# Gate/up units from inner products only: seven of seven outer products split, two units run as seven interleaved pairs, ScalarE seeds PSUM with running sums

## The chip, the cores and the metric

The kernel runs on one core of a Trainium2 chip. The metric is device time in microseconds (us) of one launch, the median of several runs. Engine names are those of the profile: PE is TensorE's matmul stream and PEld its weight loads, DVE is VectorE, ACT is ScalarE, POOL is GpSimd, and SP is the engine whose queue issues nearly all DMAs. Everything is fp32.

## The reference

One layer: a layer norm, then linear attention and a mixture-of-experts feed-forward block on the same normed input, both added to the residual. The change touches the gate and up projections of the feed-forward block only:

```
xn = layernorm(x)                                  # x: 2 x 1024 x 512
w  = routing weights of 8 experts, two kept        # sigmoid scores, top 2
gate = xn @ W_gate + lora(xn, shared) + sum_e w_e * lora_e(xn)   # 512 -> 1376
up   = xn @ W_up   + the same with its own factors
hidden = silu(gate) * up
out  = hidden @ W_down + ...                       # 1376 -> 512
x + attention(xn) + out
```

The shared low-rank factors are folded into the weights; the experts' factors stay as a matmul with a contraction of 64 rows (8 experts by rank 8).

## The kernel before

**Stages.** Up to 236 us of the profile the kernel norms and transposes x, does keys, queries, routing and the odd columns of the feed-forward block. From 236.2 to 512.1 us it does the gate and up projections. After that it does the down projection, the attention output and the residual.

**A unit.** The middle stage has ten units: five pairs of 128-column blocks `j` of the weights, times two batches `b` of 1024 tokens. A unit has to form a 2 by 2 block product (gate and up by two halves, 512 tokens by 512 tokens, contraction 512). It uses the Strassen-Winograd scheme: seven outer products `p` = 1 to 7 in place of eight. An outer product is itself a 2 by 2 block product. Five of the seven (1, 6, 2, 5, 3) are again done with seven inner products each (class `Inner`): 35 matmuls of 128 rows by 128 columns over 256 tokens. The other two (7 and 4) are done plainly by `product`: 8 matmuls over 512 tokens, accumulated in the held PSUM banks `b0` and `b1`. Eight matmuls over 512 tokens and 64 rows (`low_rank`) add the experts' part, into the banks `b`, `x` and `y`. In fp32 every matmul is two instructions on PE.

**Inner.** Inner product numbers 1 to 7 are weights `WI` times tokens `TI`; 1 and 2 use raw blocks, the others sums of blocks. Products 1, 6, 5 and 3 run up one PSUM region `ua`: after each of them ACT copies the running sum into an SBUF tile `r`, and the next accumulates on it. Products 7 and 4 run up a second region `lo`, product 2 has its own region `x_`. DVE adds `x_` and twice `lo` to the tiles. So PE may overwrite `ua` only when ACT has copied it, and may put product 4 on `lo` only when DVE has added product 7 from it:

```
        def c_sum(self):
            nc.vector.tensor_add(self.r[1][:, H1], self.r[1][:, H1], self.lo)

        def d(self):
            self.mm(self.lo, 4)
```

**Order.** PE, DVE, ACT and POOL are scheduled by hand: each runs its instructions in the order in which the program writes them (`manual_schedule`). `unit` writes the order of a unit out: inner products of two outer products alternate, with plain products and low-rank matmuls between. DVE then adds the outer products together (`add`, L1290, 128 by 512, most with both inputs in SBUF, some with one in PSUM), multiplies silu(gate) by up (L1278), and SP stores the result `h` to DRAM.

**Sums for the inner products.** Token sums are made once for each batch and outer product, weight sums once for each `j`. `next_pair(j)` hooks the work for the next `j` into the units: `fold_pe` (PE, contraction of 8 rows) and `fold_adds` (DVE, L978) fold the shared factors into the weights, `fold_sums` (DVE, L982 to L985, 128 by 256) makes the outer weight sums, `inner_weight_sums` (L1182 to L1185) the inner ones, for outer products 1, 5 and 6 on DVE and for 3 and 2 on POOL. Of the token sums, those for batch 0's products 1, 5 and 6 are made on DVE ahead of the stage, the rest on POOL in the first unit (L1138, L1160 to L1163).

**Banks.** PSUM has eight banks in this stage: `held0` to `held3`, `ab0`, `ab1`, `x0`, `x1`.

Of the kernel before, what the change touches and what calls it, by code (L numbers as in the profile page):

```python
# [10 lines left out]
F32 = mybir.dt.float32  # L11
# [4 lines left out]
P = 128  # L16
# [21 lines left out]
def layer_kernel(  # L38
# [129 lines left out]
    ad_sb = const.tile([P, FULL + 1, LR], F32, name="ad_sb")  # L168
# [66 lines left out]
    wT = [const.tile([P, BT], F32, name=f"wT{b}") for b in range(NBATCH)]  # L235
# [369 lines left out]
    def weights_across(b):  # L605
# [6 lines left out]
        nc.sync.dma_start(out=w_dram[b].rearrange("e t p -> t e p"), in_=wx)  # L612
        for i in range(2):
            for e in range(E):
                k = i * ER + e * RANK
                nc.sync.dma_start(
                    out=wT[b][k : k + RANK, :],
                    in_=w_dram[b][e].rearrange("t p -> (t p)").partition_broadcast(RANK),
                )
# [513 lines left out]
    def sums_of_four(eng, src, to):  # L1133

        b11, b12 = src[:, :, 0, 0:TH], src[:, :, 0, TH:TB]
        b21, b22 = src[:, :, 1, 0:TH], src[:, :, 1, TH:TB]
        for k, x, y in ((0, b12, b11), (1, b22, to[:, :, 0]), (2, b22, b12), (3, b21, to[:, :, 1])):
            eng.tensor_sub(to[:, :, k], x, y)  # L1138
            yield

    def inner_tokens(b, ps, t):

        for i, p in enumerate(ps):
            raw = tsum[b][p]
            TI[b, p] = {1: raw[:, 0, 0:TH], 2: raw[:, 1, 0:TH], 3: raw[:, 1, TH:TB],
                        4: t(i, 3), 5: t(i, 0), 6: t(i, 1), 7: t(i, 2)}

    def token_sums_56(eng, b, t):
        yield from sums_of_four(eng, tsum_pair[b], t)
        inner_tokens(b, (5, 6), lambda i, k: t[:, i, k])  # L1150

    def token_sums_23(b, t):
        yield from sums_of_four(nc.gpsimd, xnT[b][1].rearrange("p k (g n) -> p g k n", g=2), t)
        inner_tokens(b, (2, 3), lambda i, k: t[:, i, k])

    def token_sums_1(eng, b):
# [7 lines left out]
        inner_tokens(b, (1,), lambda i, k: t[:, k // 2, k % 2])  # L1164

    WI = {}

    def inner_weight_sums(eng, j, ps):

        w = [t.rearrange("p s (k m) -> p s k m", m=P) for t in wsum[j][0]]  # L1170
        if ps == (3,):

            slots_ = slice(5, 6)
            to = [w[k // 2][:, A21 : A21 + 1, k % 2] for k in range(4)]
        else:
            one = ps == (2,)
            slots_ = slice(1, 2) if one else slice(0, 6, 2)
            wi = p3.tile([P, 1, 4, P], F32, tag="wi2", name=f"wi2_{j}") if one else slot(5, [4, 4, P], f"wi{j}")
            to = [wi[:, 0 : len(ps), k] for k in range(4)]
        g, u = (t[:, slots_] for t in w)  # L1180
# [17 lines left out]

    class Inner:


        def __init__(self, j, b, p, tag, n):
            self.of = (j, p), (b, p)
            self.n, self.name = n, f"{p}_{tag}"

        def mm(self, out, n, start=False):
            w, t = WI[self.of[0]][n], TI[self.of[1]][n]
            nc.tensor.matmul(out, w, t, start=start, stop=True, skip_group_check=True)  # L1208

        def a(self):  # L1210
            self.r = [u_tile(f"r{m}_{self.name}") for m in range(2)]
            ab, x_ = (
                ps_pool[0].tile([P, 2, TH], F32, tag=f"{t}{self.n % 2}", name=f"{t}{self.name}") for t in ("ab", "x")
            )
            self.ua, self.lo, self.x_ = ab[:, 0], ab[:, 1], x_[:, 0]

            self.mm(self.ua, 1, start=True)
            nc.scalar.copy(self.r[0][:, H0], self.ua)  # L1218
            self.mm(self.x_, 2, start=True)

        def a_sum(self):
            nc.vector.tensor_add(self.r[0][:, H0], self.r[0][:, H0], self.x_)

        def b(self):
            self.mm(self.lo, 7)
# [953 lines left out]
```

## Time and profile before

| what | value |
|---|---|
| median of 3 runs | 721.93 us (720.92 to 722.11) |
| profiled execution: span from first to last instruction | 719.1 us |
| what lies around the span (median less span; the page gives no total of its own for this execution) | 2.8 us |
| granted TensorE clock | 1.000 |
| PE busy, DVE busy, ACT busy, POOL busy | 99%, 81%, 28%, 20% of the span |
| gate/up stage | 236.2 to 512.1 us: 275.9 us |
| its five column pairs `j` start at | 236.23, 290.30, 344.77, 399.24, 453.70 us |

A matmul's recorded duration runs to its modelled end, which lies after the next matmul's start: the pace of PE is read from the starts of successive matmuls, not from the mean duration. The chain of waits puts 84% of the span on PE and 13% on DVE.

### The profile page before, as it was taken

What the parts mean: (1) busy time and instruction counts of PE and PEld (TensorE: products, weight loads), DVE (VectorE), ACT (ScalarE), POOL (GpSimd) and SP (SyncE); (2) the same over time, 40 slices, a digit from 0 to 9 for tenths busy, and PEclk for the clock granted to TensorE, in tenths of its full rate; (3) what the DMA queues carried; (4) which work ended last, traced back from release to release, by engine and by line L of the source; (5) the groups of instructions that cost most, each with busy time, mean ns of one, the idle gap of its engine ahead of it and who ended that gap; (6) DMA issues with size and microseconds to landing.
All of it is one profiled execution on the core that took longest, in us unless ns stands there. A gap on an engine that the chain in (4) does not pass through costs nothing.

```text
span 719.1 us, 9872 instructions
## 1 busy us (share of the span) xinstructions
PE 712.2 (99%) x3410; PEld 488.9 (68%) x3410; DVE 581.7 (81%) x1331; ACT 198.2 (28%) x438; POOL 143.0 (20%) x176
## 2 busy tenths in 40 slices
PE   8999999999999999999999999999999999999998
PEld 6666675454433666666666566566788899899897
DVE  7888776777688678778778778878988789998884
ACT  4434413553532233233333333333100000000000
POOL 4033011101001842112212211534520100000000
PEclk9999999999999999999999999999999999999999
DMA  6243001115584100310210211343662444533101
GB/s 179 99 139 103 0 1 59 40 33 150 136 225 130 32 31 30 90 61 31 88 59 30 88 52 37 118 145 119 205 198 102 128 161 131 153 105 110 59 16 45
DMA packets 61734, 66.85 MB, mean 93 GB/s; under 512 B 10866, under 2 KB 49522, under 8 KB 61428
## 3 DMA queue, kind: packets, MB, share of 16 engines
q1 hardware_dynamic: 61154, 66.20, 30.1%
q8 instruction: 27, 0.44, 0.3%
q14 instruction: 23, 0.19, 0.1%
q10 hardware_dynamic: 530, 0.02, 0.0%
HBM read 44.11 MB, written 22.09 MB: 92 GB/s over the span
## 4 chain that ended last, share of the span: by engine, by line
PE 84%; DVE 13%; ACT 2%; issue 1%; POOL 0%; DVEq 0%; POOLq 0%
PE ab L1208 16%; PE b L1268 8%; PE po L1956 7%; PE pg L410 5%; PE pqu L781 4%; PE pya L1785 4%; PE pxa L1785 4%; PE pyb L1785 3%; PE ph L1653 3%; PE x L1208 3%; PE pxb L1785 2%; PE pyc L1785 2%; PE pxa L860 2%; PE b L1263 2%; PE pqv L781 2%; PE pr L1095 2%
## 5 line engine op out<-in xcount | busy, mean ns | idle before, releaser
L1268 PE MATMUL b<-t,w 128*128 128x512 f32 x160 | 83.2, 601 | 0.1
L410 PE MATMUL pg<-kt,xn 128*128 128x512 f32 x128 | 58.7, 594 | 0.5 <-DVE kt L354 0.5
L1290 POOL TENSOR_TENSOR r<-r,r 128x512 f32<-128x512 f32 x20 | 29.8, 1511 | 85.5 <-DVE t L1290 83.3
L1208 PE MATMUL ab<-ti,wi 128*128 128x256 f32 x180 | 45.4, 379 | 0.0
L1208 PEld LDWEIGHTS ab<-ti,w 128*128 128x128 f32 x140 | 25.1, 189 | 29.7 <-DVE r L1236 8.5
L1208 PEld LDWEIGHTS ab<-ti,wi 128*128 128x128 f32 x180 | 34.2, 190 | 13.2 <-issue 4.8
L1290 DVE TENSOR_TENSOR r<-r,r 128x512 f32<-128x512 f32 x60 | 43.2, 760 | 0.0
L1208 PE MATMUL ab<-ti,w 128*128 128x256 f32 x140 | 41.2, 387 | 0.8 <-DVE r L1236 0.4
L410 PEld LDWEIGHTS pg<-kt,xn 128*128 128x128 f32 x128 | 23.1, 190 | 22.6 <-issue 20.8
L1236 DVE TENSOR_TENSOR r<-r,ab 128x256 f32<-128x256 f32 x50 | 20.9, 418 | 21.7 <-ACT r L1233 21.0
L1241 ACT COPY r<-ab 128x256 f32<-128x256 f32 x50 | 18.6, 373 | 71.1 <-PE ab L1208 71.1
L1268 PEld LDWEIGHTS b<-t,w 128*128 128x128 f32 x160 | 29.2, 190 | 10.6 <-issue 5.9
L1244 DVE TENSOR_TENSOR r<-r,ab 128x256 f32<-128x256 f32 x50 | 20.9, 418 | 16.4 <-ACT r L1241 15.9
L1218 ACT COPY r<-ab 128x256 f32<-128x256 f32 x50 | 18.7, 374 | 48.4 <-PE ab L1208 47.1
L1956 PE MATMUL po<-wd,f 128*128 128x256 f32 x140 | 30.9, 380 | 0.1
L1229 ACT COPY r<-ab 128x256 f32<-128x256 f32 x50 | 18.6, 373 | 40.7 <-PE ab L1208 40.7
L1956 PEld LDWEIGHTS po<-wd,f 128*128 128x128 f32 x140 | 26.4, 190 | 4.4 <-issue 0.5
L1899 DVE TENSOR_TENSOR f<-f 128x256 f32<-128x256 f32 x84 | 29.4, 419 | 0.1
L1208 PE MATMUL ab<-xnT,w 128*128 128x256 f32 x100 | 29.4, 390 | 0.0
L419 POOL TENSOR_TENSOR ksum<-ksum,kt 128x512 f32<-128x512 f32 x12 | 15.8, 1318 | 63.1 <-DVE lg L456 42.7
L1208 PE MATMUL ab<-xnT,wi 128*128 128x256 f32 x100 | 28.1, 379 | 0.0
L1208 PEld LDWEIGHTS ab<-xnT,w 128*128 128x128 f32 x100 | 18.1, 189 | 10.9 <-issue 5.3
(483 smaller groups left out, 1651.0 us busy)
## 6 DMA issues: line engine op xcount, KB each, us to landing
h_dram<-h SPq DMA_DIRECT2D x40, 256.0 KB
f<-h_dram SPq DMA_DIRECT2D x10, 512.0 KB
x_ring<-in_x_dram SPq DMA_DIRECT2D x16, 256.0 KB
q_dram<-qt SPq DMA_DIRECT2D x16, 256.0 KB
xr<-in_x_dram SPq DMA_DIRECT2D x16, 256.0 KB
out_dram<-xr SPq DMA_DIRECT2D x15, 256.0 KB
w<-in_w_gate_dram SPq DMA_DIRECT2D x10, 256.0 KB
w<-in_w_up_dram SPq DMA_DIRECT2D x10, 256.0 KB
```

Source lines behind the costliest of these rows:

```text
L410: nc.tensor.matmul(pg[m], xns[n][:, ts(m, P)], kt, start=(j == 0), stop=(j == TPBATCH - 1))
L781: nc.tensor.matmul(banks[c], wqs[p][:, k, ts(c, P)], tsum[b][p][:, k, :], start=(start and k == 0), stop=(k == 1), skip_group_check=True,)
L1208: nc.tensor.matmul(out, w, t, start=start, stop=True, skip_group_check=True)
L1218: nc.scalar.copy(self.r[0][:, H0], self.ua)
L1236: nc.vector.tensor_add(self.r[1][:, H1], self.r[1][:, H1], self.lo)
L1244: nc.vector.tensor_add(self.r[1][:, H0], self.r[1][:, H0], self.lo)
L1268: nc.tensor.matmul(pb[m], ws[m][:, A_OF[p], ts(k, P)], tsum[b][p][:, k, :], start=start, stop=True, skip_group_check=True)
L1290: eng.tensor_add(to[m], t[m], v[m])
L1653: nc.tensor.matmul(phs[u][g * ER : (g + 1) * ER, :], a, f[:, g, :], start=(ns[0] == 0 and n == 0), stop=(last and n == len(chunks) - 1), s ...
L1785: nc.tensor.matmul(o, lhsT, rhs, start=first, stop=True, skip_group_check=True)
L1899: op(t[:, at, :], t[:, x_, :], t[:, y, :])
L1956: nc.tensor.matmul(ps[p][:, q, :], lhsT, rhs, start=start, stop=stop, skip_group_check=True)
```

## The change

All seven outer products are now `Inner` objects, so that a unit has 49 inner matmuls over 256 tokens and no plain product. The two units of one `j` (called `a` for batch 0 and `b` for batch 1) are written as seven **runs** of two interleaved outer products each: (a1, a6), (a7, a5), (a2, a4), (a3, b1), (b6, b7), (b2, b5), (b4, b3). A run has 14 **steps**, one inner matmul each, in the order of `STEPS`. The DVE adds of the inner products stand after the steps named in `SUMS`. All else hangs on a step of a run as a hook.

- The accumulation of outer products in PSUM is replaced by seeds: ACT copies a running sum (128 by 512) from SBUF into a held bank, and the low-rank matmuls accumulate onto it. Six such copies a unit, none before.
- The combination takes 4 adds of SBUF tiles on DVE and 2 on POOL, and 8 adds that read a held bank (`read`) on DVE. The multiply by up moves from DVE to POOL (`store`), all but the last two.
- All inner weight sums in the stage move to POOL, those of the first `j` for products 1, 6 and 7 excepted. There are now sums for products 7 and 4 as well. Token sums for products 7 and 4 of both batches are new: three of these four sets stand on DVE inside the first `j`.
- The fold of the next `j` is one group of matmuls after run 1, its DVE adds follow in run 2, `fold_sums` in run 3.
- Tiles: 14 `u` tiles (10 before), `wT` and `ad_sb` now live in pools that are freed before the stage; the routing weights and the down factors are loaded again (`w4`, `ad_4`) behind it, 34 DMAs on SP.

The core of the diff (hooks are written as run: {step: what}; the `return` is that of `next_fold(j)`, `start` is joined to the hooks of the first `j` only, and `end` is the last `j`, with the folds of the down weights):

```diff
     class Inner:
...
+        def banks(self, n):
+            self.ua = spare_bank(f"ab{n}", f"ab{self.name}")[:, H0]
+            x_ = ps_pool[0].tile([P, 2, TH], F32, tag=f"x{n}", name=f"x{self.name}")
+            self.x_, self.lo = x_[:, 0], x_[:, 1]
+
+        def mm(self, n):
             w, t = WI[self.of[0]][n], TI[self.of[1]][n]
+            out = {2: self.x_, 7: self.lo, 4: self.lo}.get(n, self.ua)
+            nc.tensor.matmul(out, w, t, start=n in (1, 2), stop=True, skip_group_check=True)
+            if n in (1, 6, 5, 3):
+                m, h = {1: (0, H0), 6: (1, H0), 5: (1, H1), 3: (0, H1)}[n]
+                nc.scalar.copy(self.r[m][:, h], self.ua)
+
+        def add(self, n):
+            m, h, v = {2: (0, H0, self.x_), 7: (1, H1, self.lo), 4: (1, H0, self.lo)}[n]
+            nc.vector.tensor_add(self.r[m][:, h], self.r[m][:, h], v)
+
+    STEPS = ((0, 1), (1, 1), (0, 2), (0, 6), (1, 2), (1, 6), (0, 7), (0, 5), (1, 7), (1, 5), (0, 3), (0, 4), (1, 3), (1, 4))
+    SUMS = {3: (0, 2), 5: (1, 2), 9: (0, 7), 11: (1, 7), 12: (0, 4), 14: (1, 4)}
+
+    def pair(x, y, hooks={}):
+        two = Inner(*x), Inner(*y)
+        for n, (k, p) in enumerate(STEPS, 1):
+            if n <= 2:
+                two[k].banks(k)
+            two[k].mm(p)
+            if n in SUMS:
+                k, p = SUMS[n]
+                two[k].add(p)
+            for f in hooks.get(n, ()):
+                f()
...
+        prev = {}
+        if before:
+            prev = {
+                1: [before.read(4, "b", (0,)), before.read(3, "x", (0,))],
+                5: [before.read(4, "b", (1,)), before.read(3, "x", (1,))],
+                6: [before.silu(4)], 11: [before.silu(3)], 12: [before.store(4)], 14: [before.store(3)],
+            }
+        run(1, (a, 1), (a, 6), prev)
+        run(2, (a, 7), (a, 5), {
+            1: [a.sum(V, 6, 1)],
+            11: [a.seed("x", 1, (0,))], 13: [a.seed("x", 1, (1,))],
+        })
+        run(3, (a, 2), (a, 4), {
+            1: [a.sum(V, 7, 6), a.sum(G, 6, 5)],
+            6: [a.seed("b", 7, (0,))], 11: [a.seed("b", 7, (1,))],
+            14: [a.low_rank(("x", 0, 0), ("b", 1, 1))],
+        })
+        run(4, (a, 3), (b, 1), {
+            1: [a.read(2, "x", (0,)), a.read(5, "b", (0,))],
+            5: [a.read(2, "x", (1,)), a.read(5, "b", (1,))],
+            6: [a.seed("x", 6, (0,))], 11: [a.seed("x", 6, (1,))],
+            13: [a.silu(2), a.store(2)],
+            14: [a.silu(5), a.store(5), a.low_rank(("b", 1, 2), ("x", 0, 1))],
+        })
+        run(5, (b, 6), (b, 7), {
...
+        run(6, (b, 2), (b, 5), {
+            1: [b.sum(V, 6, 1, (0,)), b.sum(V, 7, 6, (0,))],
+            5: [b.sum(V, 6, 1, (1,)), b.sum(V, 7, 6, (1,))],
...
+        run(7, (b, 4), (b, 3), {
+            1: [b.sum(G, 6, 5), b.read(2, "x", (0,))],
...
+        return {
+            1: {14: [pe]},
+            2: {5: [adds(0), adds(1)], 14: [adds(2), adds(3)]},
+            3: {5: [lambda: fold_sums(j, 0)], 14: [lambda: fold_sums(j, 1)]},
+            5: {14: [w_sums(G, j, (1,))]},
+            6: {1: [w_sums(G, j, (7, 6))], 14: [w_sums(G, j, (3,))]},
+            7: {14: [w_sums(G, j, (2, 5)), w_sums(G, j, (4,))]},
+        }
...
+    start = {
+        1: {1: [all_of(token_sums_of, V, 0, 7, spare0)], 5: [all_of(token_sums_of, V, 0, 4, spare1)]},
+        3: {1: [lambda: token_sums_1(G, 1)],
+            9: [all_of(token_sums_of, V, 1, 7, [ti23[1][:, 6], ti23[1][:, 7], ti_1[:, 6]])]},
+        4: {1: [all_of(token_sums_56, G, 1, ti_1)]},
+        5: {1: [all_of(token_sums_23, G, 1, ti23[1])],
+            14: [all_of(token_sums_of, G, 1, 4, [ti_1[:, 7 + k] for k in range(3)])]},
+    }
...
+    end = both_units(NP - 1, before, {
+        1: {14: [folds[0][0]]},
+        2: {5: [folds[0][1]], 14: loads((load_down, 2, 0))},
...
+        5: {7: [folds[1][0]], 9: [folds[1][1]], 12: [folds[2][0]], 14: [folds[2][1]]},
+        6: {14: [lambda: feature_sums(0, 0)]},
+        7: {12: [lambda: feature_sums(0, 1)], 14: [lambda: feature_sums(0, 2)]},
     })
...
+    for b in range(NBATCH):
+        spread_weights(b, w4[b])
     first_unit(hr0)
```

`V` is DVE and `G` is POOL. `token_sums_of` is four DVE subtractions of 128 by 256 with both inputs in SBUF. `unit`, `product`, `hidden` and `next_pair` are gone.

## The prediction

> **What bounds the kernel now.** I read the busy times first, then the gate/up stage in the table by stretches, then the PE timeline for the pace of a matmul, then the DVE, ACT and POOL timelines for what a late add does to PE.
>
> ```profile
> PE 712.2 (99%) x3410; PEld 488.9 (68%) x3410; DVE 581.7 (81%) x1331; ACT 198.2 (28%) x438; POOL 143.0 (20%) x176
> PE 84%; DVE 13%; ACT 2%; issue 1%; POOL 0%; DVEq 0%; POOLq 0%
> L1290 DVE TENSOR_TENSOR r<-r,r 128x512 f32<-128x512 f32 x60 | 43.2, 760 | 0.0
> ```
> ```profile
> 236.20:512.10 275.90, 275.05 (x1107) 177.78 (x1106) 223.69 (x436) 95.60 (x239) 87.87 (x90) 1.00 0.23 72
> ```
>
> The second fence has PE, PEld, DVE, ACT and POOL busy in the stage. PE is full and DVE follows with 81%. PE's chain ends everything, so the change is worth what it takes from PE's stream, less the time for which it makes PE wait. The pace:
>
> ```profile
> 272.57 0.59 PE L1208 MATMUL ab<-t,wi 128*128 128x256 f32 x2
> 273.09 1.13 PE L1263 MATMUL x<-xa,bgu_sb 64*128 64x512 f32 x4
> 274.05 1.02 PE L1263 MATMUL b<-xa,bgu_sb 64*128 64x512 f32 x4
> 275.01 1.12 PE L1268 MATMUL b<-t,w 128*128 128x512 f32 x2
> ...
> 282.01 1.02 PE L1268 MATMUL b<-t,w 128*128 128x512 f32 x2
> 282.87 0.59 PE L1208 MATMUL ab<-ti,w 128*128 128x256 f32 x2
> 283.30 0.59 PE L1208 MATMUL ab<-t,wi 128*128 128x256 f32 x2
> ```
>
> Start to start, a plain matmul (512 tokens) takes 0.86 us and an inner one (256 tokens) 0.43: the pace goes by columns, though the mean durations (601 and 380 ns an instruction) would make the narrow one look dear. A group of low-rank matmuls costs 2.1 us (273.00 to 275.01, and 0.1 more in the first matmul behind it).
>
> What a late DVE add costs:
>
> ```profile
> 501.54 0.70 PE L1208 MATMUL ab<-ti,w 128*128 128x256 f32 x2 [0.45 <-DVE r L1236]
> ```
> ```profile
> 280.46 0.42 DVE L1236 TENSOR_TENSOR r<-r,ab 128x256 f32<-128x256 f32 x1 [0.21 <-ACT r L1233]
> 280.80 0.42 DVE L982 TENSOR_TENSOR w<-w 128x256 f32<-128x256 f32 x1
> 281.13 0.42 DVE L983 TENSOR_TENSOR w<-w 128x256 f32<-128x256 f32 x1
> 286.55 1.29 DVE L1182 TENSOR_TENSOR wi<-w 128x384 f32<-128x384 f32 x1
> 291.68 0.55 DVE L1184 TENSOR_TENSOR wi<-w,w 128x384 f32<-128x384 f32 x1
> ```
> ```profile
> 515.48 0.94 DVE L1527 TENSOR_TENSOR f<-f 128x256 f32<-128x256 f32 x1
> 528.92 0.42 DVE L1527 TENSOR_TENSOR f<-f 128x256 f32<-128x256 f32 x1
> ```
>
> PE stood 0.45 us for `c_sum` (L1236), the add that frees `lo` for product 4. The other lines price DVE work with both inputs in SBUF: 128x256 takes 0.42 alone and 0.94 while POOL works, 128x384 takes 0.55 and 1.29. Adds that read PSUM keep 0.41 to 0.42 (L978, 8 of 40 beside POOL).
>
> **PE's stream.** A `j` now has 98 inner matmuls, 98 x 0.431 = 42.2 us, four low-rank groups, 8.4, and one fold group (0.85 for 8 instructions at 242.3, 0.64 more for the other 8), 1.5: 52.1. Before, the first `j` took 54.07 and the next three 54.47 (starts in the table), so 2.0 + 3 x 2.4 = 9.1 go. The last `j` has three groups of down folds of 1.27 (488.93 to 490.09, and 0.1): 50.6 + 3.8 = 54.4 against 58.4 (453.70 to 512.14), 4.0 gone. In all **-13.1 us** if PE never waits.
>
> **The new wait.** In a run PE has only the two outer products' inner matmuls to do; the plain matmuls that lay between are gone. After step 8 (product 5), ACT's copy starts 0.63 us after the matmul (283.30 to 283.93) and takes 0.37; DVE's add of product 7 follows 0.03 later (280.43 to 280.46) and takes 0.42; PE goes on 0.05 later (501.49 to 501.54): 1.50 us. Step 12 (product 4) comes 4 x 0.43 = 1.72 later, slack **0.22 us**. DVE runs its program in order, so all hooked before that add counts: the hooks of step 14 of the run before and of steps 1 and 5. From the last add of the run before (0.19 us into the run) to the end of the slack (4.05 + 0.22) is 4.1 us; less three small adds at 0.335 apart, **3.0 us** are free for hooks. The low-rank group ahead of runs 4, 5 and 7 (run 1 too, from the `j` before) adds 2.1, the fold group ahead of run 2 1.5. So only runs 3 and 6 are tight, and a late add holds the whole of PE behind it.
>
> Run 3: eight ops of 128x256 at 0.335 (four fold adds, `fold_sums` of one weight) and two of 128x512 at 0.60: 3.9, over by 0.8 even alone. POOL's `sum(G,6,5)` starts in the middle (two of 1.27 to 1.72 us) and lies beside `fold_sums`; at 0.87 apart for half or all of these it is 1.5 or 2.3. I take 1.5. Run 6: four 128x512 of SBUF, 2.4 alone, which fits; beside POOL (weight sums, stores) 0.87 to 1.17 apart, over by 0.5 to 1.6. The same 128x512 adds beside POOL took 0.68 as often as 0.95, so I take 0.3. ACT: a silu and two seeds stand ahead of run 6's first copy, 0.1. The trace has no copy into PSUM; rows on both sides are the 128x512 copies out of it (0.60) and silu (0.63), I take 0.60, and every other seed then fits between copies. Sum **1.9** for each of three `j` (0.9 to 3.5): 5.7.
>
> First `j`, run 1: DVE comes free 2.4 us into the run (the last `hr` multiply, 237.66 to 238.62), then has eight new token sums, two adds, and the add of product 7 with its release (0.47): alone 2.4 + 2.7 + 0.7 + 0.5 = 6.2 against 4.74, 1.5 late; at 0.87 apart 5.8 late. POOL is busy throughout in the trace of before (235.8 to 257.4 almost without a gap) and gets more: 4.0. Run 3: 1.5, and four token sums at step 9, 0.8 to 3.0, taken 1.5. Run 6 0.4. Run 7: POOL's queue holds token sums, weight sums, stores and `sum(G,6,5)`; the seeds wait for that, ACT's copies behind them: 0 to 3, taken 0.6. Sum **8.0** (3.1 to 15).
>
> Last `j`: run 2 has 4 x 0.60 of down folds at step 5, 0.8. In run 5 a fold group at step 7 waits for the banks that `read` empties (0.8), one at step 12 for DVE's four adds (0.9). Then seeds for run 6 wait for these banks, and run 6's first copy stands behind them on ACT: 1.5. The first down products need held banks that DVE reads last, 0.5. Sum **4.5** (3 to 8).
>
> **What costs nothing.** DVE's multiply moves to POOL: 8 a `j` at 1.27 to 1.72 (POOL adds; it has no multiply in the trace). With 4 sums and 20 weight sums POOL has 26 to 42 us of 54, and `h` is wanted much later; without that cover it is the third rival. The 34 reloads go on SP at 0.293 us an issue, 10 us. SP stood blocked behind the `h` stores up to 525.39 before, these come earlier now, and the routing weights are wanted at 548.2, the down factors at 530.7; if the cover fails, DVE's sums behind them slip, some 3 us.
>
> Total: -13.1 + 5.7 + 8.0 + 4.5 = +5.1 on the span of 719.1, so 724.2, with the 2.8 between span and median **727.0**. With all bounds low 8.8 us of waits (717.6), with all high 33.5 (742).
>
> One rule to weigh against a row is that of the Trainium skill, "SBUF — State Buffer", section "Who interferes with whom": a DVE instruction with two SBUF inputs contends with a GpSimd instruction that reads SBUF, and the pair of ports is locked for a whole instruction, not shared. This trace agrees on which adds suffer, not on the price, since 128x512 adds beside POOL took 0.97 in the mean, not 0.68 + 1.27. By the page as an estimate each of run 3's six and run 6's four adds could wait out a POOL op, which would put the total near 735.
>
> **Rivals.** *PE's count wins (715).* If the sums happen to fall beside idle POOL, or DVE's small adds are released sooner than I think, only the waits that follow without contention remain, at most 8.8 of 13.1: 709 to 718. For it: DVE had 52 us without work in the stage (275.9 less 223.7) and its work per `j` falls (four multiplies a unit and the 128x384 sums leave). It holds if run 3's wait is under 1 us and the first `j` loses under 4. *POOL bounds the first `j` (735).* There POOL has 47 to 68 us of work (28 token sums more) in 60; if it falls behind, seeds, ACT's copies and the low-rank group wait, up to 8 us. Against it: nothing of it is wanted at once but `sum(G,6,5)`. *Nothing to see (721.9).* Waits of 13 us cancel the gain.
>
> **How the numbers follow.** About 0.2% is what a measurement of this kernel tells from no change. Forecast (slower by 3 to 12 us) 0.50, PE's count wins 0.28, POOL bounds 0.14, nothing to see 0.08: faster 0.28, same 0.08, slower 0.50 + 0.14 = 0.64. The range reaches to 712 in the first rival and 738 in the second.
>
> **What would show it.** Right: starts of inner matmuls still 0.43 apart; PE waits in `mm`, released by the DVE add, most at step 12 of run 3 and in the first `j` (over 60 us long); the middle `j` 53 to 56 us; DVE's SBUF adds longer in the mean than 760 ns. Wrong: `j` at 52 to 53 us each, no DVE waits on PE, or waits of PE on ACT or POOL instead.

## The result, and the profile after

The changed kernel took **746.07 us** (median of 4 runs, 744.33 to 747.93) against 721.42 for the kernel before beside it (720.88 to 722.11): ratio 1.0341, 95% interval 1.0321 to 1.0360. It is slower, as forecast, by 24.7 us and not by 5.1; 746 lies outside the range of 712 to 738. The profiled execution took 745.56 us with a span of 743.8.

The page of the changed kernel: busy time by engine, the shares of the chain of waits, and DVE's running sums, whose 946 ns in the mean answer to 760 before.

```profile
PE 712.9 (96%) x3530; PEld 511.9 (69%) x3530; DVE 569.3 (77%) x1313; ACT 256.0 (34%) x578; POOL 220.9 (30%) x270
...
PE 80%; DVE 12%; POOL 2%; ACT 2%; issue 1%; DMA 1%; SPq 0%; DVEq 0%; ACTq 0%; POOLq 0%
...
L1279 DVE TENSOR_TENSOR r<-r,r 128x512 f32<-128x512 f32 x40 | 37.0, 946 | 1.1 <-DVE r L1279 0.5
```

The table by stretches (busy time of PE, PEld, DVE, ACT, POOL, then the granted clock): the whole gate/up stage, its first `j`, and a middle `j`.

```profile
237.17:535.04 297.87, 274.63 (x1227) 200.23 (x1225) 218.78 (x423) 153.86 (x380) 171.65 (x192) 0.99 0.20 65
237.17:306.08 68.91, 57.02 (x245) 39.98 (x243) 50.82 (x92) 30.85 (x76) 50.36 (x54) 0.95 0.09 26
361.93:417.01 55.08, 53.06 (x247) 39.89 (x245) 40.44 (x82) 30.67 (x76) 27.85 (x33) 1.00 0.18 58
```

The stage lasts 297.9 us, 22.0 more than the 275.9 of before, and PE was busy for 274.6 of them: PE went from full to waiting. POOL's work in the stage doubled (87.9 to 171.7 us), and in the first `j` PE was granted 0.95 of its clock. PE's waits in the stage, from the view of waits (total us, times, longest):

```profile
PE x L1237 <- DVE r L1244: 21.2, 19, 3.3
PE ab L1237 <- ACT r L1240: 1.7, 2, 1.3
PE po L1987 <- POOL kvo L1391: 1.0, 1, 1.0
```

So it is one wait nearly throughout: `mm` (L1237) onto a bank called `x`, released by DVE's `add` (L1244). Run 3 of a middle `j` shows how it comes about. DVE first, from the end of run 2 on, then POOL, then PE:

```profile
375.94 1.41 DVE L1555 TENSOR_TENSOR w<-w,pf 128x256 f32<-128x256 f32 x4
377.26 1.29 DVE L1279 TENSOR_TENSOR r<-r,r 128x512 f32<-128x512 f32 x2
378.46 0.75 DVE L1244 TENSOR_TENSOR r<-r,x 128x256 f32<-128x256 f32 x2
379.12 0.84 DVE L986 TENSOR_TENSOR w<-w 128x256 f32<-128x256 f32 x1
379.88 1.49 DVE L987 TENSOR_TENSOR w<-w 128x256 f32<-128x256 f32 x1
381.30 0.41 DVE L988 TENSOR_TENSOR w<-w 128x256 f32<-128x256 f32 x1
381.74 0.42 DVE L989 TENSOR_TENSOR w<-w 128x256 f32<-128x256 f32 x1
382.08 0.74 DVE L1244 TENSOR_TENSOR r<-r,x 128x256 f32<-128x256 f32 x2
```
```profile
378.09 3.00 POOL L1279 TENSOR_TENSOR r<-r,r 128x512 f32<-128x512 f32 x2 [8.53 <-DVE r L1279]
```
```profile
378.94 0.70 PE L1237 MATMUL x<-xnT,wi 128*128 128x256 f32 x2 [0.78 <-DVE r L1244]
...
382.55 0.70 PE L1237 MATMUL x<-ti,w 128*128 128x256 f32 x2 [1.19 <-DVE r L1244]
...
384.04 1.13 PE L1301 MATMUL x<-xa,bgu_sb 64*128 64x512 f32 x4
```

PE stands twice. The wait before 382.55 is the forecast one: step 12 (product 4) waits for the add of product 7 (382.08), behind `fold_sums` (L986 to L989), and of its four adds two took 0.84 and 1.49 us beside POOL's running sum, where 0.42 is what they take alone. The wait before 378.94 was not forecast: step 7 (product 7) waits for the add of product **2** (378.46), behind four fold adds (L1555) and a running sum. Measured as lateness against the pace of 0.431, it is 0.95 and 1.35 us.

Durations by `j`, between the first inner matmuls in PE's timeline (a matmul's record is missing in the kernels not listed):

| kernel | first | second | third | fourth | last | stage |
|---|---|---|---|---|---|---|
| before | 54.07 | 54.47 | 54.47 | 54.46 | 58.44 | 275.9 |
| after | 68.91 | 55.85 | 55.07 | 55.07 | 62.97 | 297.9 |
| without sum(G,6,5) | 62.56 | 53.62 | 53.61 | 53.62 | 60.75 | 284.2 |
| POOL idle in the pairs | 58.05 | 53.67 | 53.40 | 53.40 | 60.37 | 278.9 |
| without token sums of 7 and 4 | 61.85 | 55.07 | 55.07 | 55.06 | 62.98 | 290.0 |
| fold_sums late | 66.83 | 54.93 | 54.14 | 54.14 | 62.96 | 293.0 |
| other bank (and fold_sums late) | 80.98 | 66.06 | 66.07 | 66.27 | 76.53 | 355.9 |
| fold adds early | 68.81 | 55.77 | 54.99 | 54.99 | 64.66 | 299.2 |
| sum(G,6,5) at step 14 | 68.72 | 55.85 | 55.07 | 55.07 | 62.99 | 297.7 |
| hooks by windows | 64.94 | 54.55 | 53.77 | 53.97 | 62.97 | 290.2 |
| windows, POOL early | 64.45 | 52.46 | 53.09 | 53.09 | 59.32 | 282.4 |
| pairs in the middle only, second try | 56.2 | 58.3 | 53.2 | 53.5 | 58.7 | 279.9 |

### The profile page after: what moved, and what is told of

Read it like the earlier page. It is cut to its first block, busy times and chain, and to the rows that moved or that the text cites. A ratio compares the mean times of both kernels' runs of the same rounds, so it can differ in the third digit from the quotient of the medians.

```text
span 743.8 us, 10514 instructions
## 1 busy us (share of the span) xinstructions
PE 712.9 (96%) x3530; PEld 511.9 (69%) x3530; DVE 569.3 (77%) x1313; ACT 256.0 (34%) x578; POOL 220.9 (30%) x270
## 4 chain that ended last, share of the span: by engine, by line
PE 80%; DVE 12%; POOL 2%; ACT 2%; issue 1%; DMA 1%; SPq 0%; DVEq 0%; ACTq 0%; POOLq 0%
PE ab L1237 14%; PE x L1237 11%; PE po L1987 6%; PE pg L410 5%; PE pqu L785 4%; PE pya L1816 3%; PE pxa L1816 3%; PE pyb L1816 3%; PE ph L1684 3%; PE b L1301 2%; PE x L1301 2%; PE pxb L1816 2%; PE pyc L1816 2%; PE pxa L864 2%; PE pr L1099 2%; PE pqv L785 2%
## 5 line engine op out<-in xcount | busy, mean ns | idle before, releaser
L1240 ACT COPY r<-ab 128x256 f32<-128x256 f32 x280 | 103.7, 373 | 141.1 <-PE ab L1237 129.5
L1244 DVE TENSOR_TENSOR r<-r,x 128x256 f32<-128x256 f32 x210 | 86.1, 419 | 61.3 <-PE x L1237 39.7
L1322 POOL TENSOR_TENSOR r<-r,r 128x512 f32<-128x512 f32 x38 | 48.8, 1294 | 85.6 <-ACT r L1315 81.9
L1237 PE MATMUL ab<-ti,wi 128*128 128x256 f32 x200 | 60.1, 382 | 1.6 <-ACT r L1240 1.3
L410 PE MATMUL pg<-kt,xn 128*128 128x512 f32 x128 | 58.7, 594 | 0.5 <-DVE kt L354 0.5
L1237 PE MATMUL x<-ti,w 128*128 128x256 f32 x120 | 37.3, 393 | 11.6 <-DVE r L1244 11.5
L1237 PEld LDWEIGHTS ab<-ti,wi 128*128 128x128 f32 x200 | 37.4, 190 | 9.3 <-ACT r L1240 3.1
L1279 DVE TENSOR_TENSOR r<-r,r 128x512 f32<-128x512 f32 x40 | 37.0, 946 | 1.1 <-DVE r L1279 0.5
L1279 POOL TENSOR_TENSOR r<-r,r 128x512 f32<-128x512 f32 x20 | 27.0, 1369 | 30.1 <-DVE r L1279 30.1
L1311 DVE TENSOR_TENSOR r<-r,b 128x512 f32<-128x512 f32 x40 | 27.3, 683 | 9.6 <-PE b L1301 7.1
L1237 PEld LDWEIGHTS x<-ti,w 128*128 128x128 f32 x120 | 21.7, 191 | 18.7 <-DVE r L1244 11.3
L1311 DVE TENSOR_TENSOR r<-r,x 128x512 f32<-128x512 f32 x40 | 26.9, 683 | 5.3 <-PE x L1301 5.3
L1237 PE MATMUL x<-xnT,w 128*128 128x256 f32 x100 | 29.9, 380 | 0.6 <-DVE r L1244 0.6
L1315 ACT ACTIVATE r<-r 128x512 f32<-128x512 f32 x40 | 24.7, 631 | 5.5 <-DVE r L1311 5.5
L1237 PE MATMUL x<-t,wi 128*128 128x256 f32 x80 | 23.9, 380 | 2.0 <-DVE r L1244 2.0
L1843 ACT COPY wa<-pxa 128x128 f32<-128x128 f32 x9 | 2.4, 265 | 65.2 <-PE pxa L1816 58.7
L1237 PE MATMUL ab<-xnT,wi 128*128 128x256 f32 x80 | 23.9, 380 | 0.4 <-ACT r L1240 0.4
```

Source lines behind the costliest of these rows:

```text
L410: nc.tensor.matmul(pg[m], xns[n][:, ts(m, P)], kt, start=(j == 0), stop=(j == TPBATCH - 1))
L1237: nc.tensor.matmul(out, w, t, start=n in (1, 2), stop=True, skip_group_check=True)
L1240: nc.scalar.copy(self.r[m][:, h], self.ua)
L1244: nc.vector.tensor_add(self.r[m][:, h], self.r[m][:, h], v)
L1279: eng.tensor_add(self.r[to][m], self.r[to][m], self.r[of][m])
L1311: V.tensor_add(self.r[p][m], self.r[p][m], getattr(self, f"{what}{m}"))
```

## The experiments

Each is an edit of the changed kernel unless it says otherwise. Three of them leave work out to price it, four move one thing, and the others try to rebuild the order by what was found. The kernel before took 721.1 to 721.6 us beside them.

**What POOL costs.** The running sum of products 6 and 5 goes.

```diff
-    1: [a.sum(V, 7, 6), a.sum(G, 6, 5)],
+    1: [a.sum(V, 7, 6)],
...
-    1: [b.sum(G, 6, 5), b.read(2, "x", (0,))],
+    1: [b.read(2, "x", (0,))],
```

> Left out of the computation: POOL's sum(G,6,5) of both units, so the two parts of the result that need product 5 in the running sum are without it. Theory of the lock (adds with two SBUF inputs are lengthened by POOL): run 3's hooked adds, 0.6 to 0.95 us now, return to 0.42 (128x256) and 0.68 (128x512), and run 3's wait of 2.3 us in a middle j falls to 0.8 or less, about what my sum gave without contention; in the last j the feature sum of 3.39 us beside it becomes 0.42 to 1.0 and the 2.14 us wait in run 7 mostly goes. In all 6 to 9 us less: 737 to 740. Rival (the place of the hooks alone counts, POOL does not matter): run 3's wait stays at 2 us or more, under 2 us gained.

Measured 732.36 us (731.13 to 734.76; 1.0162 of before, interval 1.0141 to 1.0182): 13.7 us less, more than the 6 to 9 expected. First the group of `fold_sums`' second add in the changed kernel, then the same group here (busy time, mean ns), then PE's wait in the stage here.

```profile
L987 DVE TENSOR_TENSOR w<-w 128x256 f32<-128x256 f32 x8 | 7.6, 952 | 0.0
```
```profile
L987 DVE TENSOR_TENSOR w<-w 128x256 f32<-128x256 f32 x8 | 4.4, 554 | 0.0
```
```profile
PE x L1237 <- DVE r L1244: 11.8, 13, 2.5
```

Run 3 of a middle `j` is down to 7.09 us: the 1.35 at step 12 are gone, the 0.95 at step 7 stayed to the hundredth. Four instructions a `j` fewer, on an engine that PE never waits for here, gave 6.3 us in the first `j`, 1.5 to 2.2 in each middle one and 2.2 in the last, where the 2.14 us wait of run 7 went. Not all of the 6.3 is adds on DVE made longer: about 2.0 are waits of run 3, 1.7 a wait in run 7 for the sum itself, and 2.4 the clock, which stays at 1.00 here (both under the first `j` below).

Then all of POOL's tensor work in the pairs goes.

```diff
 def w_sums(eng, j, ps):
-    return lambda: list(inner_weight_sums(eng, j, ps))
+    ...  # WI[j, p] names raw weights
 def sum(self, eng, to, of, ms=(0, 1)):
-    for m in ms:
+    for m in ms if eng is V else ():
 def store(self, p, eng=None):
-    (eng or G).tensor_mul(h, h, self.r[p][1])
+    if eng:
+        eng.tensor_mul(h, h, self.r[p][1])
 ...  # token sums on G: TI names raw tokens
```

> Left out of the computation: all tensor work of POOL hooked into the pairs (its running sum, the products silu x up before the stores, the sums of weights for the next j, four sets of token sums); the names point at raw weights and tokens, and PE, ACT and DVE keep all their instructions. Theory (what PE waits for is DVE's adds, and about half of that is POOL's doing): DVE's 128x512 adds fall from 946 ns in the mean to about 700, the middle j to 52.5 to 53.5 us, the last to 58 to 60, the first to 58 to 62, so 727 to 733 in all: waits of the size of my low bounds, 8.8 us, and those of the first j. Rival (waits follow from PSUM banks and the order of steps alone): middle j stay at 55, total above 740.

Measured 725.12 us (724.88 to 725.69; 1.0051, interval 1.0036 to 1.0066). The time is below the 727 to 733 expected. DVE's 128x512 adds (L1279) came down from 946 to 752 ns, where about 700 was expected. The third and fourth `j` fell to 53.4, only 0.2 less than without the running sum alone: there POOL's multiplies and weight sums cost PE next to nothing. And with POOL idle the stage still takes 278.9 us, 3.0 more than before the change: of the 35 us that the five `j` lose against PE's stream (262.8 us by the prediction's sum), 16 are not POOL's.

**What the token sums of the first `j` cost.**

```diff
-    1: {1: [all_of(token_sums_of, V, 0, 7, spare0)], 5: [all_of(token_sums_of, V, 0, 4, spare1)]},
+    1: {1: [lambda: names_of_6(0, 7), lambda: names_of_6(0, 4)]},
...  # those of batch 1 in the same way
```

> Left out of the computation: the token sums for products 7 and 4 (both units); the names point at the sums of product 6, so these two products are made of the wrong tokens by the same number of matmuls. Theory (the first j is long because twelve token sums of DVE stand ahead of the adds that PE waits for, and the clock falls behind those waits): the first j falls from 68.9 to 59 to 62 us, its waits in run 1 to under 2 and in run 3 to the 2.3 of the middle j, its granted clock rises from 0.95 to 0.99 or more; the other j keep their times. In all 7 to 10 us less: 736 to 739. Rival (POOL's queue, or the last routing multiply on DVE, bounds the first j): under 3 us gained, and PE's waits there name POOL or ACT.

Measured 738.63 us (735.97 to 740.14): 7.4 less, all of it in the first `j` (61.9 where 68.9). Run 1 fell from 9.90 to 6.70 us, the 3.5 at step 14 of run 3 and the 1.7 of run 7 went. The rest of the excess there (run 3 keeps 3.4, run 4 gets 2.1) is left without these token sums. The clock still fell to 0.50 there, for 3.41 us where it had been 6.83.

**Which order DVE works in.** Both `fold_sums` at one later place.

```diff
-    3: {5: [lambda: fold_sums(j, 0)], 14: [lambda: fold_sums(j, 1)]},
+    3: {14: [lambda: fold_sums(j, 0), lambda: fold_sums(j, 1)]},
```

> Both weights' fold_sums stand at step 14 of run 3, ahead of run 4 and its low-rank group, where one of them stood at step 5 of run 3. Theory (PE waits for DVE's add of product 7, and that add waits for whatever is hooked before it in DVE's program): the 1.35 us wait at step 12 of run 3 goes, the 0.95 at step 7 stays, so run 3 falls from 8.55 us to about 7.2 in the middle j; run 4 has 2.1 us more room and takes the four adds with under 0.3 us of new wait. First j some 1.5 less, no change in the last. In all 5 to 6 us less: about 740.5. Rival (PE waits because DVE has too much to do around run 3, wherever it is hooked): the wait moves to run 4 and the time stays at 744 to 746.

Measured 744.08 us (742.72 to 745.63). Run 3 did what was expected, 8.55 to 7.09 with 0.95 left at step 7; run 4 took 0.43 of it back; the middle `j` gained 0.93 each. The total gained 2.0 of the 5 to 6 us: the stage gave 4.9, but the down stage took 210.6 us where it had taken 208.8, with a wait of 1.6 us for a DVE result (`had`) that the trace of the changed kernel does not have.

On top of that edit, product 7 and product 4 go to the second half of the bank of product 1, away from product 2.

```diff
-    self.ua = spare_bank(f"ab{n}", f"ab{self.name}")[:, H0]
+    ab = spare_bank(f"ab{n}", f"ab{self.name}")
+    self.ua, self.lo = ab[:, H0], ab[:, H1]
     x_ = ps_pool[0].tile([P, 2, TH], F32, tag=f"x{n}", name=f"x{self.name}")
-    self.x_, self.lo = x_[:, 0], x_[:, 1]
+    self.x_ = x_[:, 0]
```

> Nothing is left out. The kernel with both fold_sums at step 14 of run 3, and one thing more: products 7 and 4 go to the second half of the bank of product 1, no longer beside product 2. Theory (step 7 waits since product 7's half shares a bank's tile with product 2's, which DVE still has to read): the 0.95 us wait at step 7 of run 3 in the middle j goes without any hook being moved, and so does the 0.43 at step 7 of run 4; in their place product 3 at step 11 may wait 0.2 us or less for the add of product 7. Run 3 of the middle j 6.15 to 6.6 us against 7.09. Rival (step 7 waits for something else that DVE does late, such as the sums that feed it): 0.95 stays.

Measured 802.25 us (801.38 to 805.06). The expectation was right on step 7, where no wait is left in any run of a middle `j`, and wrong on the price. The waits of PE in the stage:

```profile
PE ab L1238 <- ACT r L1241: 34.2, 72, 1.0
PE ab L1238 <- DVE r L1245: 12.2, 11, 3.4
```

Now product 4 follows product 3 into the same bank and waits 0.63 us for ACT to copy the *other half* out, twice a run, and product 3 waits 0.22 or more at step 11; every run lasts 7.93 us where it lasted 6.15. The wait goes with the bank that two halves share, whichever the halves are. This is the rule of the Trainium skill, "PSUM — Partial Sum Buffer", section "PSUM bank collisions raise a hardware error": an access of one engine is to be held off another's by bank (and 32-partition quadrant), not by address. The runs show what waiting by bank costs, 0.95 us in one layout and 0.63 in the other; none was run without it.

Next, the fold adds that stood ahead of run 3.

```diff
-    2: {5: [adds(0), adds(1)], 14: [adds(2), adds(3)]},
+    2: {5: [adds(0), adds(1), adds(2), adds(3)]},
```

> All four fold adds stand at step 5 of run 2; two of them stood at step 14, right ahead of run 3, which has no low-rank group before it. Theory (PE waits for the add of product 2 at step 7 of run 3 because DVE still has 1.34 us of hooks from step 14 ahead of it): the 0.95 us wait at step 7 goes; the add of product 7 is reached 1.3 us sooner too, so the sum of run 3's waits falls from 2.3 to about 1.0, the middle j from 55.07 to 53.8, run 2 keeps 6.15. In all about 5 us less: 740 to 742. Rival (step 7 waits for the bank that the two halves share, whatever DVE has queued): 0.95 stays and the time with it.

Measured 745.93 us (744.25 to 748.62): nothing gained. Step 7 of run 3 lost its wait, as expected; but run 2 now waits 1.14 us at step 12. DVE there, and the late matmul of run 3 after it:

```profile
370.80 0.42 DVE L1244 TENSOR_TENSOR r<-r,x 128x256 f32<-128x256 f32 x1 [0.44 <-PE x L1237]
371.14 2.73 DVE L1555 TENSOR_TENSOR w<-w,pf 128x256 f32<-128x256 f32 x8
373.79 0.75 DVE L1244 TENSOR_TENSOR r<-r,x 128x256 f32<-128x256 f32 x2
```

From these runs the room is measured. Hooks of step 5: 2.65 us of them (371.14 to 373.79) made 1.14 of wait, and 2.61 made 1.09 in run 3 (this kernel), so **1.5 us** are free. Hooks of step 14 and step 1: 2.52 us (375.94 to 378.46 in the changed kernel) made 0.95, so **1.6 us** are free, and 1.21 us made none. Two windows, and what is free in one does not help the other.

POOL's running sum, hooked later, behind run 3.

```diff
-    1: [a.sum(V, 7, 6), a.sum(G, 6, 5)],
+    1: [a.sum(V, 7, 6)],
...
-    14: [a.low_rank(("x", 0, 0), ("b", 1, 1))],
+    14: [a.sum(G, 6, 5), a.low_rank(("x", 0, 0), ("b", 1, 1))],
```

> POOL's sum(G,6,5) of the first unit is issued at step 14 of run 3, not at step 1; run 4's adds on DVE read PSUM, which POOL did not lengthen (683 ns in every kernel so far). Nothing is left out. Theory (that sum costs by lying beside DVE's adds of two SBUF inputs): the middle j come down as without the sum, from 55.07 to 53.6, the first j by 4 to 6 us; the last j keeps its 2 us in run 7, where the other unit's sum stays. In all 8 to 11 us less: 735 to 738. Rival (the sum is late wherever it is, since the read of product 5 in run 4 has to wait until POOL has read that tile): run 4 waits 1 us or more, the middle j stay at 54.6 or above.

Measured 747.10 us (747.03 to 748.08): no gain, and no test of the theory, since the edit did not move the sum. The rival's 54.6 or more in the middle `j` came true, its wait in run 4 did not. POOL's line in the third `j`:

```profile
376.85 3.00 POOL L1279 TENSOR_TENSOR r<-r,r 128x512 f32<-128x512 f32 x2 [8.53 <-DVE r L1279]
```

The `j` starts 1.24 us earlier than in the changed kernel (360.69 and 361.93), and so does the sum (376.85 and 378.09): it lies at the same moment of run 3. The place of a hook orders an instruction in its engine's own queue; POOL's queue had nothing else in it, so the sum began when DVE's running sum (L1279) released its operands, 8.5 us after POOL had fallen idle, wherever the hook stood.

**Rebuilding the order.** Both edits together, with two plain products in the first `j` in place of token sums.

```diff
+    AS_IS = {(0, 0, 7), (0, 0, 4)}
-    two = Inner(*x), Inner(*y)
+    two = [Plain(u, p) if (u.j, u.b, p) in AS_IS else Inner(u, p) for u, p in (x, y)]
```

> The two edits before together, and in the first j products 7 and 4 of batch 0 are plain matmuls of 512 tokens (2 x 0.86 us more on PE), so that their token sums are made by POOL at its end; those of batch 1 for 7 and 4 are made by DVE ahead of the low-rank groups behind runs 4 and 6. Nothing is left out. Theory: run 3 of the middle j has no wait, 6.15 us, and these j take 52.3 to 52.6; the first j 55 to 58; the last j 60 to 62 (its folds and feature sums are as they were). In all 719 to 726. Rival (DVE has too little room in a run whatever the order, so the waits move on to runs 4 and 6): middle j 53.5 or more, total above 730.

Measured 739.82 us (738.10 to 742.17), a miss, and the rival's 730 or more: of the two edits it builds on, one had moved a wait and the other had moved nothing (1.14 in run 2 and 1.08 in run 3 are still there).

The last `j` is reordered on top of that; the diffs of this kernel and of those below are long, and only the one by windows is shown.

> The kernel before this one in the list, with the last j reordered too: its down folds in groups of two banks ahead of which a low-rank group lies (runs 4, 5, 7; the rest's group behind run 7), the running sum of products 6 and 1 on POOL there, the feature sums behind the last add. Nothing is left out. Theory (the 6 to 8 us that the last j loses are adds of folds and features ahead of DVE's add of products 7 and 2): the last j 55 to 57 us where it took 63.0, all else as in the kernel before; total 714 to 720, below the kernel before the change. Rival (the folds have to wait for banks that DVE reads last, wherever they are): the last j stays at 60 or more, the total above 720.

Measured 741.83 us (740.26 to 744.03). The stage fell to 286.7 us, but the start of the down stage lost what the last `j` gained:

```profile
PE po L2019 <- DVE r L1344: 5.2, 1, 5.2
```

DVE's last reads of the held banks (L1344, `read`) stood behind the three feature sums moved out of run 7 (523.18 to 532.09), and the down products waited for those banks. The rival's total above 720 came true, but not by the wait that it named: it is the down products that wait for the reads, not the folds.

Then the hooks placed by the two windows.

```diff
+    2: {1: [adds(0)], 5: [adds(1), adds(2)], 11: [adds(3)]},
+    3: {14: [lambda: fold_sums(j, 0)]},
+    4: {14: [lambda: fold_sums(j, 1)]},
```

> Nothing is left out; hooks of the next j's fold are placed by two windows in each run. Worked out from the runs so far: hooks of step 14 and step 1 have about 1.6 us before PE waits at step 7 (more by the low-rank or fold group ahead, 2.1 or 1.5), hooks of step 5 have about 1.55 us before PE waits at step 12, and room left in one window does not help the other. So: fold adds one at step 1, two at step 5, one at step 11 of run 2; fold_sums at step 14 of runs 3 and 4, each ahead of a low-rank group; the seeds of run 5 at steps 9 and 13. Theory of the windows: run 2 2.1 + 0.7 in 3.1 and 1.34 in 1.55, run 3 0.7 + 1.2 in 1.6 to 2.1 and nothing at step 5, runs 4 and 5 1.2 + 1.34 in 3.7: no wait of PE but 0.3 us at most in run 3; middle j 52.2 to 52.6 us where they took 55.07, the first j 2 to 5 less, the last unchanged; 732 to 738 in all. Rival (POOL's running sum or DVE's reads hold runs 4 and 5 then): middle j 54 or more, the time above 741.

Measured 739.84 us (738.81 to 742.15). Runs 2, 3 and 4 of the middle `j` have no wait left, as worked out. But the `j` take 53.8 to 54.6 us and not 52.2 to 52.6: `fold_sums` behind run 4 lies beside POOL's multiplies for the stores and took 1.49 and 1.48 us for two of its adds; run 5 waits 1.11. The total missed the 732 to 738 as well, just short of the rival's 741.

The first and the last `j` are reordered too:

> Nothing is left out; the same windows, and for the first j two plain products with the token sums of batch 1 for products 7 and 4 at step 14 of runs 3 and 6, the folds' sums later, and for the last j its down folds one pair of banks at a time, feature sums behind step 12 and ahead of the last reads. Theory of the windows: middle j 52.2 to 52.6, the first 56 to 60 (POOL still lengthens DVE's adds there), the last 55 to 57, the first down products wait 2 us or less; total 715 to 721, at or below the kernel before the change. Rival (what is taken out of one j's waits comes back where the stage ends): the last j or the wait of the first down products lose 5 us or more, total above 724.

Measured 734.98 us (733.10 to 736.04), above the 715 to 721 expected; its middle `j` took 55.2, 53.7 and 53.7. Its first `j` waited 2.12 us for token sums queued behind `fold_sums` on DVE, and PE's pace behind that wait is worth seeing:

```profile
289.25 0.59 PE L1237 MATMUL x<-t,w 128*128 128x256 f32 x2
291.96 0.85 PE L1237 MATMUL ab<-ti,wi 128*128 128x256 f32 x2 [2.12 <-DVE ti L1141]
292.61 1.06 PE L1237 MATMUL x<-xnT,w 128*128 128x256 f32 x2
293.46 1.06 PE L1237 MATMUL ab<-ti,w 128*128 128x256 f32 x2
```

Start to start the pairs are 0.85 us apart, twice the 0.43, up to 298.7.

All products are inner again, with more of the sums on POOL and earlier:

> Nothing is left out, all products inner. Against the kernel with plain products: POOL makes the token sums of the first j itself, those of products 7, 2, 3 and 4 of batch 0 ahead of the stage, where it stood idle for 13.9 us (it waited for DVE to free the memory of one weight sum that now comes later in its queue); its weight sums for the next j come behind its running sum in run 7, so that POOL is idle in runs 5 and 6; fold_sums of both weights at steps 11 and 14 of run 3; down folds of the last j in groups that share PE time. Theory of the windows, and of POOL beside DVE: middle j 52.2 to 52.8 us, the first 54 to 60, the last 57 to 59, the stage 268 to 276 against 275.9 before the change; 714 to 724 in all. Rival (POOL is now late itself: the sums of weights for products 1 and 6 are wanted in run 1 of the next j, those of tokens in runs 3 to 5 of the first): PE's waits name POOL, middle j above 54 or the first above 62, 728 or more.

Measured 731.75 us (731.00 to 731.97). The middle `j` are where the theory puts them, 52.46 and 53.09 us, 1.4 to 2.0 **below** the kernel before; one of them has 0.29 us of wait, so 52.2 us is PE's stream by itself. The first `j` is not: 64.45, with waits of 1.56 and 1.44 in run 1 and a clock of 0.95, where 54 to 60 were expected. The stage took 282.4 where 268 to 276 were expected, and the down stage 211.0, 4.0 more than before. The rival's 728 or more came true, but PE's waits name DVE, not POOL.

So the last two make only the three middle `j` from pairs, and the first and the last unit by unit as before.

> Nothing is left out. The first and the last j are made unit by unit as before the change (products 7 and 4 plain); the three j between are pairs with the windows of the kernel before in this list; the token sums of products 7 and 4 are made by POOL beside the first j's second unit. Theory (the pairs gain where nothing but pairs runs, and what the change lost sits in the first j, the last j and the start of the next stage): first j 54 to 55.5, middle j 52.4 to 53.2, last j 58 to 60 (it reads the last pairs' sums first), the next stage as before; 714 to 719, faster than before the change by 0.3 to 1 percent. Rival (the pairs' gain of 1.4 to 2 us a j is lost again where the two orders meet, or the clock falls there): 720 to 724.

Measured 732.17 us (731.25 to 733.13). One wait at the start of the second `j` took 6.8 us: eight weight sums and four token sums stood in POOL's queue ahead of the running sum that DVE, and so PE, needed. It missed the 714 to 719 and the rival's 720 to 724 alike.

The same kernel with POOL's queue in another order:

> Nothing is left out; the kernel whose three middle j alone are pairs, with POOL's queue in the first j's second unit in another order: its running sum comes ahead of eight weight sums and the token sums that had stood in front of it, and the token sums for product 7 of batch 1 move to where POOL stood idle for 9.9 us. Theory (the one wait of 6.8 us at the start of the second j, and the clock of 0.87 behind it, were that queue's): both go, the second j falls from about 63 to 53 us, the total from 732 to 718 to 721, at or just below the kernel before the change. Rival (the border of the two orders costs PE's time whatever POOL does): a wait of 3 us or more stays at the second j's start, 724 or more.

Measured 728.08 us (727.18 to 728.51; 1.0093, interval 1.0076 to 1.0110). The 6.8 us went; in the second `j` two waits of 2.3 and 2.4 us took their place (DVE's last sums of the unit before, and ACT's copies waiting for a buffer that POOL's late multiplies held). The 718 to 721 of the theory were missed and the rival's 724 or more came true, by two waits in place of one. The third and fourth `j`, 53.2 and 53.5 us, are 1.3 and 1.0 below before; the borders cost more than they give. No version that was run beats the kernel before.

## Why the prediction was wrong in size

The mechanism was right (DVE's add releases PE late, first of all in run 3), the sizes were not. Of the 19.5 us between +5.1 and +24.6, the first `j` is 8.8, the three middle ones 4.0, the last 4.0 and what lies outside the stage 2.7. The steps that failed are the room for hooks as one budget, the mean as the price of an add beside POOL, and the clock, which the sum leaves out.

**PE's stream, -13.1: right where it can be read.** A run without a wait lasts 6.15 us, 14 x 0.431 and 0.1, and PE's stream in a middle `j` is 52.2 us against the 52.1 of the sum.

**Middle `j`, 1.9 each: measured 3.7, 3.0 and 3.0.** The place was right: run 3 lost 2.5 for 1.5, and run 6 lost 0.5 (1.3 in the second `j`) for 0.3 and 0.1. The step that failed is "3.0 us are free for hooks" as one budget. It looked at step 12 alone. Products 2 and 7 share a bank, so step 7 waits too, and the 3.0 are two windows of 1.6 and 1.5. Run 3 had 2.5 and 3.0 us in them; each overran by itself. "Eight ops of 0.335 and two of 0.60: 3.9, over by 0.8" and the 1.5 taken became 2.3 of waits. That 2.3 is also the sum's value for all of it beside POOL, but by luck: two adds were lengthened, not all, and 0.95 stays without POOL's sum. Each restart costs 0.1 more.

**First `j`, 8.0 (3.1 to 15): measured 16.8, above its range.** Run 1 was sized well, 3.5 for 4.0. Run 3 was taken at 3.0 and lost 6.9, 3.5 of it at step 14, where the token sums hooked at step 9 delay the add of product 7 of the second half; with `sum(G,6,5)` away run 3 lost 4.9, without token sums 3.4. Run 6 lost 1.4 for 0.4, run 7 1.7 for 0.6. That 1.7 is POOL being late, not an add made longer: DVE's `read` (L1311) of product 5 waits 2.27 us for POOL's running sum, and PE behind it.

```profile
301.24 0.69 DVE L1311 TENSOR_TENSOR r<-r,b 128x512 f32<-128x512 f32 x1 [2.27 <-POOL r L1279]
```
```profile
302.40 0.67 PE L1237 MATMUL x<-ti,w 128*128 128x256 f32 x2 [1.37 <-DVE r L1244]
```

And one term was missing: the clock. Behind the 3.35 us wait of run 3 the low-rank group took twice its time (the second fence is the usual pace, in the third `j`; the third has the granted clock, the number behind POOL's):

```profile
267.00 1.22 PE L1237 MATMUL x<-ti,w 128*128 128x256 f32 x2 [3.35 <-DVE r L1244]
268.15 2.08 PE L1301 MATMUL x<-xa,bgu_sb 64*128 64x512 f32 x4
270.02 1.91 PE L1301 MATMUL b<-xa,bgu_sb 64*128 64x512 f32 x4
271.86 1.27 PE L1237 MATMUL ab<-xnT,w 128*128 128x256 f32 x4
```
```profile
383.52 0.59 PE L1237 MATMUL x<-ti,w 128*128 128x256 f32 x2
384.04 1.13 PE L1301 MATMUL x<-xa,bgu_sb 64*128 64x512 f32 x4
385.01 1.02 PE L1301 MATMUL b<-xa,bgu_sb 64*128 64x512 f32 x4
385.96 0.48 PE L1237 MATMUL ab<-xnT,w 128*128 128x256 f32 x1
```
```profile
264.35:265.35 1.00, 0.00 (x0) 0.00 (x0) 1.00 (x2) 0.00 (x0) 0.92 (x2) 1.00 0.00 0
265.35:272.18 6.83, 5.18 (x11) 2.00 (x12) 4.79 (x10) 0.00 (x0) 3.61 (x3) 0.50 0.00 0
272.18:273.18 1.00, 1.00 (x5) 0.88 (x5) 0.54 (x1) 0.39 (x2) 0.00 (x0) 1.00 0.00 0
```

From 267.00 to 271.86 are 4.86 us, from 383.52 to 385.96 2.44 for the same matmuls: 2.4 us, which the view of waits does not name. The rule that PE's clock halves behind idle time is in the Trainium skill, "TensorE: Matmul & The Clock Gate", section "HAM oscillation — how this bites in real kernels". It warns of gaps above about 3.4 us; here 2.1 us were enough (the wait of 2.12 us in the last lines shown of the experiments), and a lateness of 1.4 in the same kernel was not. The traces show what decides. The stretches at half clock last 3.41, 6.83 or 13.65 us, and they begin and end on a grid of 3.41 us. The waits of PE were laid over that grid in all sixteen traces, from the start of the gate/up stage to about 580 us. Each of the 18 windows at full clock in which PE waited 2.06 us or more was followed by half clock; of those with less only one was, with 1.98, and 2.01 was not enough in another. So what counts is the waiting inside one window, not the length of a wait.

**Last `j`, 4.5 (3 to 8): measured 8.5, above its range.** Run 2 (0.9 for 0.8) and run 5 (2.0 for 1.7) were right, run 6 was 2.4 for 1.5. Run 7 was not in the sum: 2.14 us, from feature sums hooked ahead of the add of product 2 while POOL worked. One add of 128x256 there, and POOL beside it:

```profile
523.71 3.39 DVE L1527 TENSOR_TENSOR f<-f 128x256 f32<-128x256 f32 x1
```
```profile
523.44 0.93 POOL L1434 TENSOR_TENSOR bd_diff<-bd_sb 128x256 f32<-128x256 f32 x1
524.33 2.49 POOL L1279 TENSOR_TENSOR r<-r,r 128x512 f32<-128x512 f32 x2
```

**Outside the stage, nothing: measured 2.7.** The stage starts 0.94 later in this execution; in the runs that share the code ahead of it, it starts anywhere from 236.10 to 237.47, so that part is spread and no cost of the change. The down stage is 1.8 longer; 1.0 of it is the wait of the first products for POOL's `block_diffs` in the waits above, since POOL's queue now holds the last running sum and multiplies; the rest stays open.

The sum with these: -13.1 + 16.8 + 9.7 + 8.5 + 2.7 = 24.6, against 24.7 between the two spans.

**What the rule and the row said of POOL.** The row had 0.97 us for a 128x512 add beside POOL, and the sum went by such means. The page's rule, that the ports are locked for a whole instruction, was weighed and put aside with "near 735". The rule fits the runs better: a 128x256 add that is caught ends 0.28 us behind POOL, in run 3 (381.37 and 381.09) as in run 7 of the last `j` (527.10 and 526.82). It goes further than the rule, since the 3.39 us outlast more than one of POOL's instructions. A mean over all adds of a line hides that the ones ahead of a waiting PE are the ones caught, in run 3 of a middle `j` because POOL's sum and DVE's hooks both follow the same running sum on DVE (L1279). With that single sum away the loss is 11 us, not 24.7.

**The rivals.** *PE's count wins* asked for under 1 us in run 3 and under 4 in the first `j`; neither held, and even with POOL idle the time is 725.1, above that rival's 709 to 718. *POOL bounds the first `j`* was wrong in its form: PE never waits for POOL itself in the stage. It was right for 1.7 us, by way of DVE in run 7, and the work that came late is the one that it excepted, `sum(G,6,5)`. For the rest POOL slows DVE, and the part of the loss that goes with POOL's work (20.9 us of time) is more than that rival gave it.

**What cost nothing.** Right for the multiplies on POOL and the weight sums in the middle `j` (0.2 us) and for the 34 reloads (PE waits for no DMA in the stage or behind it), wrong for `sum(G,6,5)`, which was counted only for what it does to run 3.

## What to carry to other kernels

An in-order engine's slack is not one budget for a stretch of work but a window between each two results that someone waits for; list every release, those by a shared bank among them, before adding up what fits. Price a two-input SBUF add beside POOL as "may wait until POOL's instruction ends", not by the mean of its line, and ask what releases the two together. A hook that moves an instruction of an otherwise idle engine moves nothing: such work must be put behind an input or behind other work of its queue. Fillers taken out of a dense stream (here the plain matmuls between the inner ones) were the slack of every other engine, so what they cost on PE is not what their removal gives.

## What the runs showed of the hardware that was not expected

A 128x256 add on DVE, 0.42 us alone, took 3.39 us while three POOL instructions followed one another without a gap. And PE's pace was halved behind a wait of 2.1 us, in one place up to 6.7 us later (291.96 to 298.7): about 3 us on top, from the starts there against 0.43 a pair. A wait of the same length, in run 7 of the last `j` of the changed kernel (527.33 to 529.48), had no such echo: an edge of the 3.41 us grid, at 528.18, cuts it into 0.85 and 1.30. With the fold adds early the same wait lay in one window but for 0.18 us, the clock was 0.50 from 529.77 on for 3.41 us, and that last `j` took 64.66 us in place of 62.97.
